# Two attention layers and an MLP on one core: biases as rows, column tiles in one gap, unsummed last weights, another order at the tail

## The chip, the core and the metric

The kernel runs on one core of a Trainium2 chip, in float32. A core has four compute engines that run side by side, each with its own instruction stream in program order: TensorE (PE) multiplies matrices, VectorE (DVE) works elementwise and reduces, ScalarE (ACT) evaluates functions such as exp, GpSimd (POOL) does small elementwise work. SyncE (SP) issues data transfers (DMAs); ACT and POOL issue some too. Data lies in SBUF; TensorE writes to PSUM, which has eight banks of 2 KB per partition, and the other engines read it from there. Engines wait for each other by semaphores.

The metric is the device time of one execution in microseconds; lower is better.

## The reference

Input x is 16 images of 256 channels and 32 x 32 positions, taken as 16 batches of 1024 tokens (S) with 256 channels (C).

```
# layer 0: attention, 4 heads of 64
qkv  = (xs @ w_proj + b_proj).reshape(B, S, 4, 192);  q, k, v = split(qkv, 3)
res  = softmax(q @ k.T * 64**-0.5) @ v
x    = res @ w_out + b_out + xs
# layer 1: attention with 8 heads of 32, then an MLP
qkv  = group_norm(x, 32 groups) @ qkv_w.T
attn = softmax(q @ k.T * 32**-0.5 + phys_bias[head]) @ v
x    = x + attn @ proj_w.T + proj_b
h    = gelu(group_norm(x) -> mlp_w1 (1024 hidden) + mlp_b1) -> mlp_w2 + mlp_b2
out  = x + h
```

## The kernel before

A batch is worked through in stages, and all of TensorE's products are in float32. The tokens are cut into NT = 2 blocks of TB = 512 columns, the channels into CC = 2 halves of 128 rows. In each batch:

- **qk_a, v_a** (L279, the helper `product`, called from qkv): layer 0's projections. ACT evicts them from PSUM with the bias `bqk` added (L715). They are computed during the batch before, except for batch 0, where they are the first thing that TensorE does.
- **Attention of layer 0** (`attention_a`): scores `s_a` (L336) in tiles of 64 x 64, exponentials `e_a` on ACT (L344), products with v `acc_a` (L357), running sums of the exponentials `es_a` on DVE (L369), and the denominators `den_a` (L388), which are products of the sums with ones, in tiles of 128 x 32. The output projection is `o` (`out_proj`, L279), with DVE adding bias and residual (L606) and taking statistics (L609).
- **The gap**: the last acc_a, the o of the first block in two halves with den_a between them, then whatever fills TensorE until the last denominators are through (the next batch's qk_a and v_a in batch 0, the MLP's hidden layer of the batch before in the others).
- **Group norm** g, then **qk_b, v_b**.
- **Attention of layer 1** (`attention_b`): four items (block, channel half), each in four units of two key blocks: scores `s_b` (L468), exponentials `e_b` (L483), products `acc_b` (L519), whose results DVE or ACT adds into `res_b` (L532, L530), sums `es_b` of the exponentials on DVE (L498), at the end of an item the denominators `den_b` (L541) from the sums, and the output projection `j` (L279).
- **Group norm** h, and the **MLP**: hidden `m` (L802) with gelu on ACT (L810), outputs `m` (L279) in eight pieces, of which two make a block of 128 x 512; DVE adds bias and residual (L825) and SP stores (L829).

PSUM is divided by hand: three double banks that rotate (`wide`) and two single banks. Bank 0 takes one head's scores and acc, bank 1 another head's scores and den.

Most stages are generators that yield once per unit. `run(stage, fill)` goes through one and places pieces of other work (`fill`: projections of the next batch, the MLP's output pieces of the one before) after chosen units. `later.after(n, f)` calls f after n more ticks, and there is a tick per unit or piece: this is how the norm's steps (`gm` for the group means, `gv` for the variances) are placed between others. Order on an engine is thus program order, but for DVE and ACT instructions that the scheduler moves unless they are pinned.

`cols[0]` is the width of product()'s column tiles: 128 is one matmul on the whole array, 32 is four matmuls on four column strips of it. It is 32 in both attentions and 128 between them.

At the start ACT's DMA queue issues three loads of `wp` (L92), `pb` (L140) and four of the pieces of `bqk` (L143); SP issues x, two of bqk (L145) and the other weights (L147). The pieces of bqk are columns: every element is 4 bytes of its own. `exp_bias` (L169, L170) turns pb into `ebias` and spreads it to `eones`. At the tail, in batch 15, three of batch 14's eight output pieces stand behind the attention; `keep_warm` (L267) issues idle matmuls while the last norm's small products are waited for. A flag, `in_range`, is taken from the sums of all denominators by a transpose `ok_row` (L967) and two DVE steps; every engine loads it (L188) and branches past `general_pass`, a second version of the kernel that does not run here.

Of the kernel before, what the change touches and what calls it, by code (L numbers as in the profile page):

```python
# [8 lines left out]
F32 = mybir.dt.float32  # L9
# [44 lines left out]
@with_exitstack  # L54
def kernel(
    ctx: ExitStack,
    tc: tile.TileContext,
    x: bass.AP,
    w_proj: bass.AP,
    b_proj: bass.AP,  # L60
    w_out: bass.AP,
    b_out: bass.AP,
    gn1_w: bass.AP,
    gn1_b: bass.AP,
    gn2_w: bass.AP,
    gn2_b: bass.AP,
    qkv_wT: bass.AP,
    proj_wT: bass.AP,
    proj_b: bass.AP,
    phys_bias: bass.AP,  # L70
    mlp_w1T: bass.AP,
    mlp_b1: bass.AP,
    mlp_w2T: bass.AP,
    mlp_b2: bass.AP,
    out: bass.AP,
):
    nc = tc.nc
    B, C, S = x.shape
    HID = mlp_w1T.shape[1]
    CC = C // P  # L80
    SB = S // P
    NT = S // TB
    HC = HID // P
    GSZ = C // GROUPS

    const = ctx.enter_context(tc.tile_pool(name="const", bufs=1))


    wp = const.tile([P, CC, 3, HEADS0, D0], F32, name="wp")
    for t in (1, 0, 2):  # L90
        for cc in range(CC):
            (nc.gpsimd if cc else nc.scalar).dma_start(  # L92
                wp[:, cc, t],
                w_proj[cc * P : (cc + 1) * P, :].rearrange(
                    "p (h t d) -> p t h d", t=3, d=D0
                )[:, t],
            )


    bqk = const.tile([P, 3, HEADS0 // 2], F32, name="bqk")  # L100
    pb = const.tile([P, HEADS1], F32, name="pb")

    ident = const.tile([P, P], F32, name="ident")
    make_identity(nc, ident)
    mhalf = const.tile([P, CC], F32, name="mhalf")
    nc.gpsimd.memset(mhalf, -0.5)
    ones = const.tile([P, D0], F32, name="ones")
    nc.gpsimd.memset(ones, 1.0)

    def load_vec(v, n, name):  # L110
        t = const.tile([P, n], F32, name=name)
        nc.gpsimd.dma_start(t, v.rearrange("(c p) -> p c", p=P))
        return t

    bo = load_vec(b_out, CC, "bo")
    g1w = load_vec(gn1_w, CC, "g1w")
    g1b = load_vec(gn1_b, CC, "g1b")
    g2w = load_vec(gn2_w, CC, "g2w")
    g2b = load_vec(gn2_b, CC, "g2b")
    pjb = load_vec(proj_b, CC, "pjb")  # L120
    m1b = load_vec(mlp_b1, HC, "m1b")
    m2b = load_vec(mlp_b2, CC, "m2b")

    def load_mat(w, name):
        k, n = w.shape
        t = const.tile([P, k // P, n], F32, name=name)
        weights.append((t, w.rearrange("(c p) n -> p c n", p=P)))
        return t

    weights = []  # L130
    wo = load_mat(w_out, "wo")
    wq = load_mat(qkv_wT, "wq")
    wpj = load_mat(proj_wT, "wpj")
    w1 = load_mat(mlp_w1T, "w1")
    w2 = load_mat(mlp_w2T, "w2")


    def load_rest():
        bp = b_proj.rearrange("(g i t d) -> i t d g", i=2, t=3, d=D0)
        nc.scalar.dma_start(pb, phys_bias.partition_broadcast(P))  # L140
        for t in (1, 0):
            for i in range(2):
                nc.scalar.dma_start(bqk[i * D0 : (i + 1) * D0, t, :], bp[i, t])  # L143
        for i in range(2):
            nc.sync.dma_start(bqk[i * D0 : (i + 1) * D0, 2, :], bp[i, 2])  # L145
        for t, w in weights:
            nc.sync.dma_start(t, w)  # L147


    gind = const.tile([P, P // GSZ], F32, name="gind")  # L150
    nc.vector.tensor_reduce(
        gind, ident.rearrange("p (g j) -> p g j", j=GSZ), AX.X, ALU.add
    )
    gavg = const.tile([P, P // GSZ, GSZ], F32, name="gavg")
    nc.vector.tensor_scalar(
        gavg,
        gind.unsqueeze(2).to_broadcast([P, P // GSZ, GSZ]),
        1.0 / GSZ,
        None,
        ALU.mult,  # L160
    )
    gavg = gavg.rearrange("p g j -> p (g j)")


    ebias = const.tile([P, HEADS1], F32, name="ebias")
    eones = const.tile([P, HEADS1, D1], F32, name="eones")

    def exp_bias():
        nc.scalar.activation(ebias, pb, AF.Exp)  # L169
        nc.vector.tensor_copy(eones, ebias.unsqueeze(2).to_broadcast([P, HEADS1, D1]))  # L170

    bvo = const.tile([P, CC], F32, name="bvo")

    in_range = const.tile([P, 1], I32, name="in_range")

    with ExitStack() as first:
        first_pass(
            first, tc, x, out,
            dict(
                wp=wp, bqk=bqk, pb=pb, bo=bo, g1w=g1w, g1b=g1b, g2w=g2w,  # L180
                g2b=g2b, pjb=pjb, m1b=m1b, m2b=m2b, wo=wo, wq=wq, wpj=wpj, w1=w1,
                w2=w2, ident=ident, gavg=gavg, mhalf=mhalf, ones=ones, eones=eones,
                bvo=bvo, load_rest=load_rest, exp_bias=exp_bias,
                in_range=in_range,
            ),
        )

    good = nc.values_load(in_range[0:1, 0:1], min_val=0, max_val=1)  # L188
    with tc.If(good == 0):
        with ExitStack() as again:  # L190
            general_pass(
                again, tc, x, out,
                dict(
                    wp=wp, bqk=bqk, pb=pb, bo=bo, g1w=g1w, g1b=g1b, g2w=g2w,
                    g2b=g2b, pjb=pjb, m1b=m1b, m2b=m2b, wo=wo, wq=wq, wpj=wpj, w1=w1,
                    w2=w2, ident=ident, gavg=gavg, mhalf=mhalf, b_proj=b_proj,
                ),
            )


def first_pass(ctx, tc, x, out, k):
# [62 lines left out]
    def keep_warm(what, n):  # L264
        ps = bank("warm", 1)
        for _ in range(n):
            nc.tensor.matmul(  # L267
                ps[:, : what.shape[1]], what[:, :P], what, start=True, stop=True
            )
# [52 lines left out]
    def attention_a(b, qT, kT, v, project):  # L322
# [102 lines left out]
        while pending:  # L425
            weigh(*pending.pop(0))
            if not pending:


                cols[0] = P  # L430
                first_half = project(0, res)
                first_half((0,))
                yield
                first_half((1,))
                break
            yield

# [6 lines left out]
    def attention_b(b, qT, kT, v, project):  # L444
# [41 lines left out]

        def add(i, kb, es, block):
            if kb == 0 and block == 0:  # L490
                sums[i] = [
                    work.tile([P, 2, TB], F32, tag="es", name=f"es_{key}_{i}_{n}", bufs=4)
                    for n in range(G // 2)
                ]
                return
            for n in range(G // 2):
                d = sums[i][n]
                ins = nc.vector.tensor_add(d, es[n] if kb == 0 else d, es[2 * block + n])  # L498
                if block:
                    tc.keep_in_program_order(ins)  # L500
# [35 lines left out]
        def normalise(i, r, last):  # L536
            t, c = items[i]
            at_end = last and b == B - 1
            den = bank(f"den_{key}_{i}", 1)
            for g in range(G):  # L540
                nc.tensor.matmul(  # L541
                    den[g * D : (g + 1) * D, :],
                    k["eones"][:, c * G + g],
                    sums[i][g // 2][:, g % 2, :],
                    start=True,
                    stop=True,
                )
            if at_end:

                full = work.tile([P, CC * TB], F32, tag="full", name="rd_end", bufs=1)  # L550
# [44 lines left out]
    def out_proj(key, w, src, bias, xs, t, stats, then):  # L595
        todo = list(range(CC))

        def issue(cos=range(CC)):
            apart = cols[0] == P
            if not apart:  # L600
                both = wide(f"{key}_{t}")
            ps = {}
# [27 lines left out]
        return issue  # L630


    def group_norm(key, src, stats, gw, gb, tag, out_tile, wait, at_end=False):
        st = {}


# [22 lines left out]
        def variances():  # L659
# [1 line left out]
            for sl, ps in averages(f"gm_{key}", st["mean_c"]):  # L661
                nc.vector.tensor_copy(mean[sl], ps)

            if at_end:
                keep_warm(k["ident"], 4)
            dv = small.tile([P, CC], F32, tag="dv", name=f"dv_{key}")
            nc.vector.tensor_sub(dv, st["mean_c"], mean)
            nc.vector.tensor_mul(dv, dv, dv)
# [5 lines left out]
        def apply():  # L674
            rstd = small.tile([P, CC], F32, tag="rstd", name=f"rstd_{key}")
            for sl, ps in averages(f"gv_{key}", st["tv"]):
                nc.vector.tensor_scalar(rstd[sl], ps, EPS, None, ALU.add)
            if at_end:
                keep_warm(k["ident"], 10)
            nc.gpsimd.tensor_tensor(rstd, rstd, k["mhalf"], ALU.pow)  # L680
            a = small.tile([P, CC], F32, tag="ga", name=f"ga_{key}")
            nc.vector.tensor_mul(a, rstd, gw)
# [113 lines left out]
    def mlp(b, xb, hn):  # L796
# [16 lines left out]
        def reduce(t, co, half):  # L813
# [11 lines left out]
            nc.vector.scalar_tensor_tensor(  # L825
                y, ps, k["m2b"][:, co : co + 1], y, ALU.add, ALU.add
            )
            if half:
                nc.sync.dma_start(  # L829
                    out[b, co * P : (co + 1) * P, t * TB : (t + 1) * TB],  # L830
                    xb[:, co, t * TB : (t + 1) * TB],
                )

        return (
            [lambda t=t, hc=hc: hidden(t, hc) for t in range(NT) for hc in range(HC)],
# [29 lines left out]
    keep_warm(nothing, 3)  # L865
    xs = {0: load_x(0)}
    k["load_rest"]()
    tiles0, (first_qk, first_v) = qkv_0(0, xs[0])

    run_pieces(first_qk[::2] + first_qk[1::2] + first_v)  # L870
    k["exp_bias"]()


# [16 lines left out]
    for b in range(B):  # L890
# [31 lines left out]
            first = []  # L922
        if b == B - 1:

            now, end = outputs[:5], outputs[5:]
        if not first:

            fill = {m: [piece] for m, piece in enumerate(own[:5:2] + own[1::2] + own[6:])}
# [11 lines left out]
        for m, pieces in enumerate(rest):  # L940
# [4 lines left out]
                b, tiles1, xs[b],  # L945
                lambda st, b=b, hn=hn: group_norm(
                    f"h{b}", xs[b], st, k["g2w"], k["g2b"], "q1", hn,
                    3 if b + 1 < B else 2, b == B - 1,
                ),
            ),  # L950
            fill,
# [305 lines left out]
```

## Time and profile before

| what | us |
|---|---|
| median of 4 runs | 3775.19 |
| lowest, highest | 3773.49, 3776.57 |
| profiled execution, its own time | 3774.78 |
| its span in the profile | 3772.9 |
| TensorE busy | 3757.0 |
| DVE busy | 2231.4 |
| ACT busy | 2034.2 |
| POOL busy | 78.0 |

The profiled execution is one of the kind that the four runs are; its time is its span and 1.9 us around it. Times within it count from the span's start. In lines of groups or of the timeline, `x16` is a number of instructions, "128\*32" the shape of the part of the array that a matmul uses, "out<-in" the tiles by name, and a bracket the idle time of the engine before the line and what ended it. In the list of waits the three numbers are the time in total, how often, and the longest. In the timeline, matmuls of one kind are merged, and the first number is the start, the second the time from the first start to the last end; a next line can start before that end, since matmuls overlap. In the chain, "ACTq" is a DMA that ACT issues.

### The profile page before, as it was taken

Reading aid. Unit: us, or ns where it says so; the run is one execution under the profiler, and the core shown is the slowest. Engines: PE = TensorE matmul, PEld = TensorE weight load, DVE = VectorE, ACT = ScalarE, POOL = GpSimd, SP = SyncE. Lnnn points to the kernel's source line nnn. Section 1 sums busy time; section 2 is a strip of 40 time slices with the busy share of each in tenths; the row PEclk is TensorE's granted clock in tenths of the full one; section 3 lists DMA queues with packets and bytes.
Section 4 is the critical chain, followed back from the end, with each engine's and each line's share of the span. In section 5 each row is a group of like instructions: output and inputs, shape, how many; then the busy total and the mean of one; then the engine's idle time right before and its main releaser. Section 6 shows DMA issues by size and latency. Waiting matters only on the chain.

```text
span 3772.9 us, 86793 instructions
## 1 busy us (share of the span) xinstructions
PE 3757.0 (100%) x38335; PEld 1491.4 (40%) x38335; DVE 2231.4 (59%) x2764; ACT 2034.2 (54%) x2624; POOL 78.0 (2%) x245
## 2 busy tenths in 40 slices
PE   9999999999999999999999999999999999999999
PEld 3334343343433434334343333433334333343335
DVE  4684656746566565665656656565565655646573
ACT  4655546555465554555546455554655556555461
POOL 1000000000000000000000000000000000000000
PEclk9999999999999999999999999999999999999999
DMA  2000000000001000000000001010000100100000
GB/s 85 12 14 13 30 13 16 27 13 30 12 16 32 7 30 13 19 29 8 30 13 23 26 10 31 8 33 15 13 30 7 33 15 13 30 7 22 15 12 22
DMA packets 63052, 78.27 MB, mean 21 GB/s; under 512 B 35820, under 2 KB 37356, under 8 KB 62668
## 3 DMA queue, kind: packets, MB, share of 16 engines
q1 hardware_dynamic: 59964, 71.85, 6.2%
q8 instruction: 302, 4.95, 0.5%
q14 instruction: 82, 0.67, 0.1%
q10 hardware_dynamic: 2304, 0.40, 0.1%
q0 software_dynamic: 400, 0.41, 0.1%
HBM read 54.28 MB, written 17.56 MB: 19 GB/s over the span
## 4 chain that ended last, share of the span: by engine, by line
PE 97%; DVE 1%; issue 1%; ACT 1%; DMA 0%; ACTq 0%; POOLq 0%; POOL 0%; DVEq 0%
PE s_b L468 13%; PE acc_b L519 12%; PE m L802 12%; PE m L279 12%; PE s_a L336 12%; PE acc_a L357 11%; PE qk_b L279 6%; PE qk_a L279 6%; PE o L279 3%; PE v_b L279 3%; PE v_a L279 3%; PE j L279 3%; PE den_b L541 1%; PE den_a L388 1%; DVE es_a L369 0%
## 5 line engine op out<-in xcount | busy, mean ns | idle before, releaser
L483 ACT ACTIVATE e_b<-s_b 128x1024 f32<-128x1024 f32 (+1 forms) x1280 | 982.6, 865 | 471.2 <-PE s_b L468 471.2
L498 DVE TENSOR_TENSOR es_b<-es_b,e_b 128x1024 f32<-128x1024 f32 x768 | 900.1, 1221 | 337.5 <-ACT e_b L483 337.4
L344 ACT ACTIVATE e_a<-s_a 128x1024 f32<-128x1024 f32 x512 | 521.2, 1025 | 359.8 <-PE s_a L336 349.4
L468 PE MATMUL s_b<-q,k 32*64 32x512 f32 x8192 | 535.8, 601 | 4.0 <-DVE res_b L532 3.3
L336 PE MATMUL s_a<-q,k 64*64 64x512 f32 x4096 | 532.6, 593 | 1.1
L357 PE MATMUL acc_a<-e_a,v 64*64 64x512 f32 x4096 | 528.5, 589 | 0.0
L369 DVE TENSOR_TENSOR es_a<-es_a,e_a 128x1024 f32<-128x1024 f32 x384 | 469.3, 1222 | 85.4 <-ACT e_a L344 73.4
L519 PE MATMUL acc_b<-e_b,v 128*32 128x512 f32 x4096 | 492.1, 598 | 0.0
L279 PE MATMUL m<-g,w 128*32 128x256 f32 (+1 forms) x7664 | 464.1, 379 | 0.0
L802 PE MATMUL m<-gn_h,w 128*128 128x512 f32 x1024 | 451.3, 595 | 0.3 <-DVE gn_h L692 0.3
L810 ACT ACTIVATE g<-m,m1b 128x512 f32<-128x512 f32 x256 | 175.9, 687 | 358.3 <-PE m L802 358.3
L279 PEld LDWEIGHTS m<-g,w 128*32 128x32 f32 (+1 forms) x7664 | 276.7, 112 | 216.8 <-issue 41.9
L468 PEld LDWEIGHTS s_b<-q,k 32*64 32x64 f32 x8192 | 174.2, 130 | 288.7 <-issue 147.1
L802 PEld LDWEIGHTS m<-gn_h,w 128*128 128x128 f32 x1024 | 192.2, 190 | 230.6 <-issue 229.8
L357 PEld LDWEIGHTS acc_a<-e_a,v 64*64 64x64 f32 x4096 | 161.9, 133 | 277.5 <-issue 236.2
L336 PEld LDWEIGHTS s_a<-q,k 64*64 64x64 f32 x4096 | 152.6, 133 | 278.1 <-issue 211.8
L519 PEld LDWEIGHTS acc_b<-e_b,v 128*32 128x32 f32 x4096 | 108.5, 109 | 351.1 <-ACT e_b L483 194.7
L532 DVE TENSOR_TENSOR res_b<-res_b,acc_b 128x512 f32<-128x512 f32 x192 | 131.2, 683 | 196.2 <-PE acc_b L519 196.2
L279 PE MATMUL qk_a<-x,wp 128*32 128x512 f32 (+1 forms) x1856 | 231.6, 592 | 3.7 <-ACT q L715 1.8
L279 PE MATMUL qk_b<-gn_g,wq 128*32 128x512 f32 (+1 forms) x1280 | 234.0, 592 | 0.0
L736 DVE TENSOR_TENSOR v<-v_b,eones 128x512 f32<-128x512 f32 x64 | 44.0, 688 | 291.2 <-PE v_b L279 291.2
L498 DVE TENSOR_TENSOR es_b<-e_b,e_b 128x1024 f32<-128x1024 f32 x128 | 150.6, 1218 | 0.0
(121 smaller groups left out, 2094.7 us busy)
## 6 DMA issues: line engine op xcount, KB each, us to landing
rd_a<-row_a SPq DMA_DIRECT2D x64, 256.0 KB
out_dram<-x SPq DMA_DIRECT2D x64, 256.0 KB
rd_b<-row_b SPq DMA_DIRECT2D x252, 64.0 KB
x<-in_x_dram SPq DMA_DIRECT2D x30, 512.0 KB
w<-in_L_conv_mlp_w_dram SPq DMA_DIRECT2D x2, 1024.0 KB
x<-in_x_dram SPq DMA_DIRECT2D x4, 256.0 KB
sp_b<-d_b SPq DMA_DIRECT2D x63, 8.0 KB
row_b<-inv_b SPq DMA_DIRECT2D x63, 8.0 KB
```

What stands on the lines that cost most here:

```text
L279: nc.tensor.matmul(o[sl], w[:, sl], r, **flags)
L336: nc.tensor.matmul(s[h : h + HALF, g, :], kT[g * D : (g + 1) * D, c, kb * P + h : kb * P + h + HALF], qT[g * D : (g + 1) * D, c, t * TB : ...
L344: nc.scalar.activation(e, s, AF.Exp, scale=float(D) ** -0.5)
L357: nc.tensor.matmul(accs[i][h][g * D : (g + 1) * D, :], v[h * HALF : (h + 1) * HALF, kb, c * 2 + g], e[h * HALF : (h + 1) * HALF, g, :], st ...
L369: nc.vector.tensor_add(sums[i], held[i] if kb == 1 else sums[i], e)
L468: nc.tensor.matmul(outs[g][h : h + HALF, :], kT[g * D : (g + 1) * D, c, k0 : k0 + HALF], qT[g * D : (g + 1) * D, c, t * TB : (t + 1) * TB] ...
L483: nc.scalar.activation(to, s, AF.Exp, scale=float(D) ** -0.5)
L498: ins = nc.vector.tensor_add(d, es[n] if kb == 0 else d, es[2 * block + n])
L519: nc.tensor.matmul(acc[g * D : (g + 1) * D, :], v[:, kb + m, c * G + g], es[2 * m + g // 2][:, g % 2, :], start=(m == 0), stop=(m == 1),)
L532: nc.vector.tensor_add(r, r, acc)
L802: nc.tensor.matmul(ps, k["w1"][:, cc, hc * P : (hc + 1) * P], hn[0][:, cc, t * TB : (t + 1) * TB], start=(cc == 0), stop=(cc == CC - 1),)
L810: nc.scalar.activation(g, ps, AF.Gelu, bias=k["m1b"][:, hc : hc + 1])
```

## The change

Four parts:

1. **Biases as rows.** The six loads of bqk columns go. Three loads bring b_proj as rows, `brow` (6 x 128), on ACT's queue between wp's second third (t = 1) and the others. TensorE turns it (a transpose to 128 x 6 in bank 0, placed behind the first two k tiles) and DVE copies it to bqk. The order of the first four tiles on TensorE becomes k, k, transpose, q, q, where it was k, q, k, q.
2. **Column tiles in the gap.** o's two halves in the gap use 128 x 32 tiles, each in a bank of its own as before; the width changes to 128 only after them.
3. **Last weights unsummed.** For items 2 and 3 of batch 0 and item 3 of batch 15 (`spared`), the last unit's exponentials are not added to the sums; den_b takes their four tiles as further rounds of its accumulation.
4. **Tail.** In batch 15 four of the output pieces stand in the attention and four behind it, where it was five and three; the last norm waits one tick less, so that its gm and gv stand between those pieces; the idle matmuls go. The last block of the output is stored in two halves. On all engines the flag's steps (ok_row and what follows from it) stand behind the last output piece, where they stood in front of the last MLP.

```diff
     wp = const.tile([P, CC, 3, HEADS0, D0], F32, name="wp")
+    brow = const.tile([3 * HEADS0 // 2, P], F32, name="brow")
     for t in (1, 0, 2):
+        if t == 0:
+            bp = b_proj.rearrange("(g i t d) -> t g i d", i=2, t=3, d=D0)
+            for u in range(3):
+                nc.scalar.dma_start(
+                    brow[u * 2 : (u + 1) * 2].rearrange("g (i d) -> g i d", d=D0), bp[u]
+                )
...
     def load_rest():
-        bp = b_proj.rearrange("(g i t d) -> i t d g", i=2, t=3, d=D0)
         nc.scalar.dma_start(pb, phys_bias.partition_broadcast(P))
-        for t in (1, 0):
-            for i in range(2):
-                nc.scalar.dma_start(bqk[i * D0 : (i + 1) * D0, t, :], bp[i, t])
-        for i in range(2):
-            nc.sync.dma_start(bqk[i * D0 : (i + 1) * D0, 2, :], bp[i, 2])
...
+                first_half = project(0, res)
+                first_half((0,), True)
+                yield
+                first_half((1,), True)
                 cols[0] = P
-                first_half = project(0, res)
-                first_half((0,))
-                yield
-                first_half((1,))
                 break
...
+        spared, apart = {0: (2, 3), B - 1: (3,)}.get(b, ()), {}
         def add(i, kb, es, block):
...
+            if i in spared and kb == SB - 2:
+                apart[i] = es
+                return
...
             den = bank(f"den_{key}_{i}", 1)
-            for g in range(G):
-                nc.tensor.matmul(
-                    den[g * D : (g + 1) * D, :],
-                    k["eones"][:, c * G + g],
-                    sums[i][g // 2][:, g % 2, :],
-                    start=True,
-                    stop=True,
-                )
+            parts = sums[i] + apart.get(i, [])
+            for m in range(0, len(parts), G // 2):
+                for g in range(G):
+                    nc.tensor.matmul(
+                        den[g * D : (g + 1) * D, :],
+                        k["eones"][:, c * G + g],
+                        parts[m + g // 2][:, g % 2, :],
+                        start=(m == 0),
+                        stop=(m + G // 2 == len(parts)),
+                    )
...
-        def issue(cos=range(CC)):
-            apart = cols[0] == P
+        def issue(cos=range(CC), apart=False):
+            apart = apart or cols[0] == P
...
-            if at_end:
-                keep_warm(k["ident"], 4)
...
-            if at_end:
-                keep_warm(k["ident"], 10)
...
-            if half:
-                nc.sync.dma_start(
-                    out[b, co * P : (co + 1) * P, t * TB : (t + 1) * TB],
-                    xb[:, co, t * TB : (t + 1) * TB],
-                )
+            each = b == B - 1 and (t, co) == (NT - 1, CC - 1)
+            if half or each:
+                sl = slice(t * TB + (half * n if each else 0), t * TB + (half + 1) * n)
+                nc.sync.dma_start(out[b, co * P : (co + 1) * P, sl], xb[:, co, sl])
...
     k["load_rest"]()
+    ps, n = bank("bqk", 0), k["brow"].shape[0]
+    turn = nc.tensor.transpose(ps[:, :n], k["brow"], k["ident"][:n, :n])
+    nc.vector.tensor_copy(k["bqk"].rearrange("p t g -> p (t g)"), ps[:, :n])
     tiles0, (first_qk, first_v) = qkv_0(0, xs[0])
-    run_pieces(first_qk[::2] + first_qk[1::2] + first_v)
+    start = first_qk[::2] + first_qk[1::2] + first_v
+    start[0]()
+    with tc.issue_after(turn.ins):
+        start[1]()
+    run_pieces(start[2:])
...
-            now, end = outputs[:5], outputs[5:]
+            now, end = outputs[:4], outputs[4:]
...
-                    3 if b + 1 < B else 2, b == B - 1,
+                    3 if b + 1 < B else 1,
```

More of the change, by code (lines that the diff above doesn't have):

```diff
@@ L182 @@
                 w2=w2, ident=ident, gavg=gavg, mhalf=mhalf, ones=ones, eones=eones,
-                bvo=bvo, load_rest=load_rest, exp_bias=exp_bias,
+                bvo=bvo, brow=brow, load_rest=load_rest, exp_bias=exp_bias,
                 in_range=in_range,
@@ L630, in out_proj, with group_norm @@
         return issue
-    def group_norm(key, src, stats, gw, gb, tag, out_tile, wait, at_end=False):
+    def group_norm(key, src, stats, gw, gb, tag, out_tile, wait):
         st = {}
```

## The prediction

> **What bounds the kernel now.** I read the page first: engine table, then the chain that ended last.
>
> ```profile
> PE 3757.0 (100%) x38335; PEld 1491.4 (40%) x38335; DVE 2231.4 (59%) x2764; ACT 2034.2 (54%) x2624; POOL 78.0 (2%) x245
> ...
> PE 97%; DVE 1%; issue 1%; ACT 1%; DMA 0%; ACTq 0%; POOLq 0%; POOL 0%; DVEq 0%
> ```
>
> TensorE is busy for 3757.0 of 3772.9 us, so 15.9 us of the span is not matmul. An edit pays if it takes passes from TensorE (one 512-column pass takes 0.43 us start to start), bubbles between passes, or part of those 15.9 us; relief on DVE or ACT is worth nothing where TensorE runs through. The waits of TensorE say where it doesn't:
>
> ```profile
> PE s_b L468 <- DVE res_b L532: 3.3, 6, 0.9
> PE qk_a L279 <- ACT q L715: 1.8, 1, 1.8
> PE qk_a L279 <- ACT k L715: 1.6, 1, 1.6
> ```
>
> The two of qk_a are the start. The chain of the first 26 us:
>
> ```profile
> 2.12 7.84 DMA wp<-in_L_conv_w_proj_dram
> 9.96 0.02 issue
> 9.98 0.60 ACTq L143
> ...
> 10.62 5.88 DMA bqk<-in_L_conv_b_proj_dram
> ...
> 16.61 0.70 ACT q L715
> ...
> 17.35 7.13 PE qk_a L279 x16
> ```
>
> ACT's third bqk load waits on a completion semaphore that the wp load shares (9.96), the last lands at 16.50, and TensorE stands: by the timeline 2.26 us (11.27 to 13.53), then 2.10 us (15.25 to 17.35). qk_a ends at 24.48.
>
> **Part 1, biases as rows.** Six loads of 4-byte pieces become three of four 256-byte pieces, ahead of two wp loads on ACT's queue; SP loses two, so wo, wq and the later loads go about 2 us sooner. An issue on that queue takes 0.60 to 0.67 us. Three put wp t=0 from 1.42 to about 3.4 and pb from 2.81 to about 4.9, where it also waits for the x block that lands at 4.89. Queue data is served in order and wp t=1 before it only lands at 4.72, so I leave wp t=0 at its landing of 7.8 and pb at its 10.2 (both read from the completion records); brow, with so few pieces and between the two, before 7 by estimate.
>
> The new order on TensorE: k, k from 5.66 to about 9.2, the transpose (which waits for brow and the identity, nothing later), q to about 11.1, then the fourth tile. It needs the first k eviction on ACT, which now waits for the bqk copy. On DVE that copy stands behind eones (waits ebias on ACT, which waits pb) and gind: pb 10.2, ebias 0.21, eones 0.29, gind 0.28, copy about 0.2: 11.4. The ACT_TABLE_LOAD (1.28) fits before pb lands. Eviction 0.69: the fourth tile starts at 12.3. No second stall follows, and the remaining five tiles take 5 x 1.72 = 8.6: end 20.9. To that I add 0.7 for hand-overs between engines and for wo and wq, which now share the DMA engines with pb: 21.6. Gain **2.9 us**. Bounds: pb landing 3 us later gives nothing (the copy would be at 14.4); pb early gives at most the 4.4 us of stalls.
>
> **Part 2, column tiles in the gap.** Once per batch, in time order:
>
> ```profile
> 88.72 1.98 PE L279 MATMUL o<-res_a,wo 128*128 128x512 f32 x4
> 90.63 1.07 PE L388 MATMUL den_a<-es_a,ones 128*32 128x256 f32 x16
> 91.63 1.98 PE L279 MATMUL o<-res_a,wo 128*128 128x512 f32 x4
> 93.45 2.74 PE L279 MATMUL qk_a<-x,wp 128*128 128x512 f32 x6
> ```
>
> Four passes are 1.72 us, yet o to den_a takes 1.91, den_a's 0.86 take 1.00 and the second o 1.82: each change of tile shape costs 0.09 to 0.11, and the first 128x128 pass after one takes 0.105 more (o: 592 median, 697 longest, ns). With 128x32 tiles o, den_a, o have one shape: 1.72 + 0.86 + 1.72 and one change plus slow pass at the end, 0.21: 4.52 against 93.45 - 88.72 = 4.73. Saved 0.21 x 16 = **3.3 us**.
>
> Against it stands a rule of the Trainium skill (TensorEngine Tiling (Array Packing), Instruction Overhead): each matmul carries about 60 cycles. The halves go from 8 records to 32 per batch; at the clock of 2.4 GHz that the skill gives (TensorE: Matmul & The Clock Gate) 24 x 25 ns x 16 = 9.6 us lost by estimate, net 6.3 lost. The row: the same product j, in both forms.
>
> ```profile
> 213.71 3.62 PE L279 MATMUL j<-res_b,wpj 128*32 128x512 f32 x32
> ...
> 3697.58 3.60 PE L279 MATMUL j<-res_b,wpj 128*128 128x512 f32 x8
> ```
>
> 24 more instructions cost 0.02 us, since four column tiles run side by side (starts 7 ns apart). I take the row: 0.3 us over 16 batches, within rounding. Range 2.3 to 3.6.
>
> **Part 3, the last weights unsummed.** Per item it drops four DVE adds (two rows of 2.35) and adds four rounds of den_b: 4 x 0.43 = 1.72 us on TensorE. Batch 0, item 2:
>
> ```profile
> 191.33 2.35 DVE L498 TENSOR_TENSOR es_b<-es_b,e_b 128x1024 f32<-128x1024 f32 x2
> ...
> 193.60 0.68 DVE L532 TENSOR_TENSOR res_b<-res_b,acc_b 128x512 f32<-128x512 f32 x1
> ...
> 194.34 1.97 PE L468 MATMUL s_b<-q,k 32*64 32x512 f32 x30 [0.92 <-DVE res_b L532]
> ...
> 197.98 1.04 PE L541 MATMUL den_b<-es_b,eones 128*32 128x512 f32 x8
> ```
>
> Without the adds res_b runs at 192.5 and the 0.92 stall goes; then den_b takes 1.72 more and everything behind it (s_b, d_b's copy, e_b) moves: +0.8. Item 3 has no stall after its spared adds (TensorE runs without a gap from 210.07 to 219.83 and on): +1.72. Its earlier 0.43 stall at 210.07 follows exponentials that come later by the same 0.8; it stays. Sum **2.4 us lost**. Bounds: if the freed DVE also removed the 0.43 and more of the stalls it would be 1.5 lost; if the chain of DVE steps (186 to 210, on the chain of this stretch) shortens by all 4.7 us of item 2's adds, 1.3 gained. e_b tiles are held until den_b, but the exponentials that reuse them come after it. Batch 15's item is in part 4.
>
> **Part 4, the tail.** Before, acc_b of 3682.71 to the first hidden matmul of the last MLP:
>
> ```profile
> 3709.95 2.03 PE L267 MATMUL warm<-ident 128*128 128x128 f32 x16
> ...
> 3712.29 1.99 PE L802 MATMUL m<-gn_h,w 128*128 128x512 f32 x4 [0.31 <-DVE gn_h L692]
> ```
>
> That is 29.6 us. After, TensorE has in this order: acc 1.72, j 3.43, acc 1.72, den 0.97 + 1.72, m 3.45, j 3.43, m 3.43, gm, m 3.43, gv, m 3.43, small products and switches 0.6: 27.4. Each step's cover: the 3.36 RECIPROCAL and the scaling of the last result lie under the first m and half of j (a stall of 0.2 at most); bn_stats to mean_c (2.65 after j) under the second m; gm to tv_h (0.9) under the third; rstd to gn_h (2.2) under the last. With that cover gone the 2.2 would be bare. Gain 29.6 - 27.4 = **2.1 us** (0.5 to 3), the 1.72 of den included. Removing the warm matmuls has a rule against it (clock-gate page, Part 1: an idle window of about 3.4 us halves the clock; worth about 3.4 us once). The granted clock is 1.00 there, and the new order leaves no such gap, so I add nothing.
>
> The very end:
>
> ```profile
> 3767.68 0.48 DVE L825 SCALAR_TENSOR_TENSOR x<-m,m2b,x 128x256 f32<-128x256 f32 x1 [2.97 <-PE m L279]
> 3768.20 0.33 SPq L829 DMA_DIRECT2D out_dram<-x  x1
> ```
>
> The store lands at 3771.02, but by the raw records DVE ends the span: it loads the flag by 3768.24, branches, and its next instruction comes 3.5 us later (3771.83). Now ok_row's transpose, least (0.28), cast (0.14) and the flag's load (0.5) follow the last x on all engines: the branch goes about **1.0 us later** (0 to 2). Halving the last store can't help: the landing is not last.
>
> **Sum.** -2.9 - 3.3 + 2.4 - 2.1 + 1.0 = -4.9. The profiled execution (3774.78, span 3772.9) becomes 3769.9; it stood 0.4 under the median of 3775.19, so the median becomes **3770.3**.
>
> **Rivals.** (a) *Larger gain*, 0.22: batch 0 is paced by DVE, whose relief gains 1.3 instead of 2.4 lost (the DVE steps on the chain speak for it, the unbroken TensorE after 210 against), and the start gets all 4.4: -4.9 - 3.7 - 1.5 = -10.1: 3765.1. (b) *Start and tail don't pay*, 0.14: pb lands 3 us late and the norm's chain stays bare: -4.9 + 2.9 + 2.1: 3775.3. pb's wait for an earlier load speaks for it, its small share of the queue against. (c) *Slower*, 0.02: the instruction overhead of 60 cycles holds in the gap: 9.6 us there, 3780 in all; it outweighs all gains from 13 ns per extra matmul and passes +0.2% from 32 ns. The j rows (0.8 ns) speak against.
>
> **How the numbers follow.** 0.2% is 7.55 us, about what a measurement of this kernel can tell from no change (the four runs spread over 3.1). The forecast has 0.62, at 3768 to 3773. (a) lies mostly beyond 3767.6, (b) within. Faster 0.23, within 0.75, slower 0.02. The range takes in (b)'s middle part and most of (a): 3765.5 to 3774.5.
>
> **What would show it.** qk_a ends near 21.6 with one stall, its releaser ACT k (pb late: after 24). o x16 at 1.72 with den_a next at 0.86. den_b at 2.6 in batch 0, with the 0.92 wait gone. Hidden's start in the last MLP 27.4 after acc, no warm. DVE's in_range after the last x. The forecast falls if den_b's rounds cost less than 0.43 each or if batch 0's attention as a whole gets shorter.

## The result and the profile after

The changed kernel takes 3770.27 us (median of 40 runs, 3768.8 to 3774.06) against 3774.4 us of the kernel before in the same sessions (60 runs): ratio 0.9988, 95% interval 0.9983 to 0.9992, about 4 us. The profiled execution took 3770.62 us, its span is 3768.8 us, 4.1 us under that of before.

The engine table of the page and the waits of TensorE (engine and line, released by; total, times, longest):

```profile
PE 3755.8 (100%) x38692; PEld 1485.3 (39%) x38692; DVE 2218.2 (59%) x2753; ACT 2034.3 (54%) x2624; POOL 77.9 (2%) x245
```

```profile
PE s_b L470 <- DVE res_b L541: 2.4, 5, 0.7
PE warm L269 <- DVE nothing L871: 1.5, 1, 1.5
PE qk_a L281 <- ACT k L722: 0.6, 1, 0.6
```

TensorE is as full as before. Of the two waits of qk_a one is left, the stall of 0.9 us in batch 0 is gone from s_b's list, and so is a wait of 0.3 us for gn_h in the tail. Where the 4.1 us come from is read by laying both timelines side by side at fixed points of TensorE's order:

| stretch | before | after | difference | forecast |
|---|---|---|---|---|
| span's start to first v_a | 24.32 | 21.88 | -2.44 | -2.9 |
| to the first s_a of batch 1 (one gap, batch 0's unsummed items) | 195.51 | 197.54 | +2.03 | -0.2 + 2.4 |
| to the first o of batch 15 (14 gaps) | 3325.01 | 3322.23 | -2.78 | -2.9 |
| to the first hidden matmul of the last MLP (one gap, the tail) | 167.44 | 165.10 | -2.34 | -0.2 - 2.1 |
| that MLP on TensorE | 55.36 | 55.26 | -0.10 | 0 |
| from its last matmul to the end | 5.27 | 6.76 | +1.49 | +1.0 |
| sum | 3772.9 | 3768.8 | -4.1 | -4.9 |

The start, by the chain of the changed kernel's first 26 us:

```profile
5.41 6.19 DMA pb<-in_L_conv_phys_bias_dram
...
11.62 0.22 ACT ebias L171
11.84 0.02 issue
11.86 0.29 DVE eones L172
12.16 0.19 DVE gind L153
12.35 0.08 DVE bqk L877
...
12.46 0.70 ACT k L722
...
13.20 8.85 PE qk_a L281 x20
22.05 4.10 PE v_a L281 x19
```

The order is the predicted one, pb, ebias, eones, gind, bqk, eviction, fourth tile; pb comes later than assumed.

The gap, in time order:

```profile
86.28 1.92 PE L281 MATMUL o<-res_a,wo 128*32 128x512 f32 x16
88.02 1.05 PE L390 MATMUL den_a<-es_a,ones 128*32 128x256 f32 x16
88.89 1.90 PE L281 MATMUL o<-res_a,wo 128*32 128x512 f32 x16
90.72 9.71 PE L281 MATMUL qk_a<-x,wp 128*128 128x512 f32 x22
```

o to den_a takes 1.74, den_a 0.86, the second o 1.83 with the one change of shape that is left: 4.43 (4.74 before), in every one of the 16 batches. Of these 0.30 us, 0.10 comes back in the first 128x128 pass, so 0.20 per batch stay (2.78 over 14 gaps).

Batch 0's second attention:

```profile
194.24 1.04 PE L552 MATMUL den_b<-es_b,eones 128*32 128x512 f32 x8
195.10 1.90 PE L552 MATMUL den_b<-e_b,eones 128*32 128x512 f32 x16
196.93 2.74 PE L470 MATMUL s_b<-q,k 32*64 32x512 f32 x32
...
217.60 1.90 PE L552 MATMUL den_b<-e_b,eones 128*32 128x512 f32 x16
219.43 2.81 PE L338 MATMUL s_a<-q,k 64*64 64x512 f32 x24
```

The rounds from e_b are the 1.72 us per item (16 records, 1.90 to the end of the last, overlapped by the next). The tail, with gv_h between two pieces of m and no warm:

```profile
3703.09 0.28 PE L281 MATMUL gv_h<-tv_h,gavg 128*128 128x2 f32 x2
3703.22 3.70 PE L281 MATMUL m<-g,w 128*128 128x256 f32 x16
3706.76 9.60 PE L809 MATMUL m<-gn_h,w 128*128 128x512 f32 x22
```

acc_b of 3679.39 to 3706.76 is 27.37 us, where 27.4 was forecast. The very end:

```profile
3761.86 0.27 PE L981 MATMUL ok_row<-ident,both 128*1 128x128 f32 x1
3762.06 0.48 DVE L832 SCALAR_TENSOR_TENSOR x<-m,m2b,x 128x256 f32<-128x256 f32 x1 [2.97 <-PE m L281]
3762.46 0.27 DVE L983 TENSOR_REDUCE least<-ok_row 1x1 f32<-1x128 f32 x1
3762.76 0.14 DVE L984 CAST in_range<-least 1x1 int32<-1x1 f32 x1
```

By the raw records every engine loads the flag at 3762.9 and branches from 3763.5 on.

No line of the diff moves the flag: in both sources its block stands behind `run_pieces(hidden + outputs)`. In the trace of before, `ok_row` runs ahead of the last MLP all the same, between two idle matmuls:

```profile
3709.04 0.27 PE L967 MATMUL ok_row<-ident,both 128*1 128x128 f32 x1
```

So the scheduler moves this product of TensorE too. The kernel with part 4 alone, whose edit does not touch the block either, has it at 3765.81, behind the last piece. It is thus an edit of part 4 that turned the order; which one was not tested.

### The profile page after: what moved, and what is told of

It is laid out like the page before. It is cut to its first block, busy times and chain, and to the rows that moved or that the text cites. A ratio compares the mean times of both kernels' runs of the same rounds, so it can differ in the third digit from the quotient of the medians.

```text
span 3768.8 us, 87484 instructions
## 1 busy us (share of the span) xinstructions
PE 3755.8 (100%) x38692; PEld 1485.3 (39%) x38692; DVE 2218.2 (59%) x2753; ACT 2034.3 (54%) x2624; POOL 77.9 (2%) x245
## 4 chain that ended last, share of the span: by engine, by line
PE 97%; DVE 1%; issue 1%; ACT 1%; DMA 0%; SPq 0%; DVEq 0%
PE s_b L470 13%; PE acc_b L528 12%; PE m L809 12%; PE m L281 12%; PE s_a L338 12%; PE acc_a L359 11%; PE qk_b L281 6%; PE qk_a L281 6%; PE v_b L281 3%; PE o L281 3%; PE v_a L281 3%; PE j L281 3%; PE den_b L552 2%; PE den_a L390 1%; DVE es_a L371 0%
## 5 line engine op out<-in xcount | busy, mean ns | idle before, releaser
L507 DVE TENSOR_TENSOR es_b<-es_b,e_b 128x1024 f32<-128x1024 f32 x756 | 885.9, 1221 | 339.1 <-ACT e_b L485 339.0
```

## The experiments

Below, "in its trace" means between the same fixed points as above, so a difference in the start does not enter another stretch. Kernels that are alike in a stretch agree in it within 0.3 us from trace to trace. Medians are of 6 to 21 runs each, and all kernels with the start of before spread over two groups of times some 2.5 us apart (a likely reason stands under part 1). The intervals of the four parts alone and of the kernel without the adds reach a ratio of 1, no change, so the verdicts on these rest on the stretches of their traces more than on the medians. Theories: **mine**, TensorE's passes and bubbles decide, part by part, and the parts add; **rival A**, DVE's relief in batch 0 is worth more than the passes it costs; **rival B**, an overhead per matmul spoils the gap; **rival C**, start or tail don't reach the end.

**Part 2 alone.** The kernel before with

```diff
+                first_half = project(0, res)
+                first_half((0,), True)
+                yield
+                first_half((1,), True)
                 cols[0] = P
...
```

> The kernel before with part 2 alone (the gap's o in 128x32 tiles, every batch). My account: 0.20 us less per batch, 3.2 us less than before in all; o to the work behind den_a and o takes 4.43 instead of 4.74 us to its first matmul, of which 0.1 comes back in that first matmul. Rival (a fixed cost per matmul of 60 cycles, 384 more matmuls): 6 us more than before.

3770.82 us against 3774.12 (ratio 0.9992, 0.9984 to 1.0000). In its trace, from the first v_a to the last matmul, 3.1 us less than before; the gap 4.43. Mine holds; 384 more matmuls cost nothing that can be seen, so rival B falls: it wanted 6 us more.

**Part 1 alone** (three row loads, the transpose and the copy; the six column loads out).

> The kernel before with part 1 alone (biases as rows). My account: the first qk_a ends 2.4 us earlier and nothing behind it takes that back, since TensorE runs through: 2.4 us less than before. Rival (the start is hidden behind something later): the difference is lost by the first gap, no change in the time.

3772.19 us against 3774.12 (0.9993, 0.9985 to 1.0001). In its trace the first v_a stands at 21.25 instead of 24.32, and the last matmul is 3.0 earlier: nothing is taken back. Rival C falls for the start. The medians differ by 1.9 us only; the trace of before is one execution of a start that varies (see below). The chain of its first 26 us shows that TensorE then has no stall at all in qk_a:

```profile
1.47 5.49 PE warm L268 x6
6.95 3.81 PE qk_a L280 x8
10.76 0.15 PE bqk L870
10.91 10.50 PE qk_a L280 x24
21.41 4.75 PE v_a L280 x22
```

The traces with the start of before do not agree among themselves: the first v_a stands at 24.32, 25.68 (part 2 alone), 23.13 (part 3), 26.22 (part 4) and 23.32 (the last one below). With the new start of part 1 it stands between 20.62 and 21.88 in seven traces. The two latest have the bqk loads late for both evictions, and TensorE idle for 2.74 and 2.65 us at once. Part 2 alone, the stall and then stretches of 2 us (the last three numbers are the granted TensorE clock, the DMA share and GB/s):

```profile
15.30 10.55 PE L279 MATMUL qk_a<-x,wp 128*128 128x512 f32 x20 [2.74 <-ACT k L715]
...
14.00:16.00 2.00, 0.70 (x2) 0.46 (x3) 0.00 (x0) 1.44 (x3) 0.00 (x0) 1.00 1.01 357
16.00:18.00 2.00, 2.00 (x4) 0.88 (x4) 0.00 (x0) 0.62 (x2) 0.00 (x0) 0.67 1.02 398
18.00:20.00 2.00, 2.00 (x3) 0.68 (x2) 0.00 (x0) 0.47 (x1) 0.00 (x0) 0.50 1.10 358
20.00:22.00 2.00, 2.00 (x6) 0.94 (x5) 0.00 (x0) 0.69 (x1) 0.00 (x0) 0.98 1.06 409
```

From 1.4 us after the stall's end the clock is half for 3.4 us, and four passes start 0.85 us apart instead of 0.43: 1.7 us more. In part 4 alone the same 3.4 us begin 0.35 us after a stall of 2.65 us. The longest stall of the other twelve traces here is 1.84 us (before), and none of them has the half clock. The Trainium skill (TensorE: Matmul & The Clock Gate, Part 1) has this rule, half rate after an idle window of about 3.4 us that runs free of the kernel; here stalls of 2.74 and 2.65 us went before it, shorter than that window, after 0.38 and 1.25 us of idle a little earlier. No run varies the stall alone, so the cause is argued from these fourteen traces. Both profiled executions with it lie in the upper group of their kernel's times (part 4 alone: seven runs at 3770.8 to 3771.6, six at 3773.6 to 3775.4, the profiled one 3774.31), the others in the lower. With part 1, 12 of 13 runs lie within 1.2 us. That each run of the upper group has the half clock was not shown run by run, and the new start does not end every spread: the 21 runs of the changed kernel with batch 0 summed again lie over 4.8 us.

**Part 3 alone, in batch 0.**

```diff
+        spared, apart = {0: (2, 3)}.get(b, ()), {}
...
+            if i in spared and kb == SB - 2:
+                apart[i] = es
+                return
...
```

> The kernel before with part 3 alone, for items 2 and 3 of batch 0. My account: 2.3 us more than before: 3.4 us of den_b passes against one stall of 0.9 us that goes. Rival (DVE paces batch 0's second attention and its relief counts): 1 us less than before or better.

3777.08 us against 3774.12 (1.0006, 0.9998 to 1.0014). In its trace the stretch from the first v_a to batch 1 grows by 2.23 us. Rival A falls. To see both halves of the bill apart, the same without den_b's further rounds (its denominators lack the last unit, so it serves for its time only):

> The kernel before without the last unit's four DVE adds in items 2 and 3 of batch 0 and without any further rounds of den_b: the last unit is left out of those denominators. What DVE's relief alone is worth. My account: only the 0.9 us stall in item 2 goes, 0.9 us less than before. Rival (DVE sets the pace from 186 to 210 us): 2.4 to 4.7 us less than before.

3772.92 us against 3774.12 (0.9996, 0.9988 to 1.0005); in its trace that stretch is 1.11 us shorter, where the rival wanted 2.4 or more. Its den_b in item 2 and what follows:

```profile
195.87 1.04 PE L546 MATMUL den_b<-es_b,eones 128*32 128x512 f32 x8
196.86 2.82 PE L468 MATMUL s_b<-q,k 32*64 32x512 f32 x32
...
207.97 1.97 PE L468 MATMUL s_b<-q,k 32*64 32x512 f32 x30 [0.43 <-DVE res_b L537]
```

So eight DVE adds (9.4 us of DVE) are worth 1.1 us, the rounds cost 1.11 + 2.23 = 3.3 us (3.44 forecast), and the 0.43 stall of item 3 stays, as the prediction had it. And undone in the changed kernel:

> The changed kernel with batch 0's last weights summed again (batch 15's still unsummed). My account: 2.3 us less than the changed kernel, 6.4 less than before. Rival (DVE's relief counts): 1 us more than the changed kernel or worse.

3768.48 us against 3774.12 (0.9983, 0.9977 to 0.9990): 5.6 us less than before (6.4 expected), where the changed kernel has 4.1. In its trace the stretch has only the gap's gain, 0.2.

**Part 4 alone, nothing unsummed.**

```diff
-            now, end = outputs[:5], outputs[5:]
+            now, end = outputs[:4], outputs[4:]
...
-                    3 if b + 1 < B else 2, b == B - 1,
+                    3 if b + 1 < B else 1,
...
```

> The kernel before with part 4 alone (four and four pieces, one tick less, no idle matmuls, halved last store), the last weights summed in batch 15 too. My account: the last MLP starts 2.8 us earlier (29.6 less the 27.4 of the changed kernel, less 1.7 for den_b's rounds, plus about 1.1 for a wait of j for the scaled result); the end after the last matmul grows by 1.5 us, since the flag is now read behind it: 1.2 us less than before. Rival (the tail pays as a whole, the end is free): 2.8 us less.

3771.61 us against 3774.12 (0.9994, 0.9985 to 1.0002). In its trace the last MLP starts 3.4 us earlier after the first o of batch 15 than before (2.8 expected) and the end grows by 1.3. By the medians this is 2.5 us less than before, twice what was expected and near the rival's 2.8, but not for the rival's reason: the end is not free. Of the expected wait of j for the scaled result, 1.1 us, only 0.24 is there: the scheduler puts the first passes of the next m into it.

```profile
3696.00 1.02 PE L279 MATMUL j<-res_b,wpj 128*128 128x512 f32 x2
3696.86 0.59 PE L279 MATMUL m<-g,w 128*128 128x256 f32 x2
3697.69 2.81 PE L279 MATMUL j<-res_b,wpj 128*128 128x512 f32 x6 [0.24 <-DVE part L555]
```

Batch 15's unsummed weights so have next to no stall to pay for them. All weights summed in the changed kernel:

> The changed kernel with all last weights summed. My account: batch 15's rounds cost 1.7 us of TensorE and save about 1.1 us of a wait of j for the scaled result, so this is 0.6 us faster than the one with batch 0 alone undone. Rival (the sparing is worth it where the reciprocal is waited for): it is 0.5 us or more slower than that one.

3767.29 us against 3774.12 (0.9981, 0.9973 to 0.9988), 1.2 under the one before; in its trace the tail, without its gap's 0.2, is 3.4 us shorter than before, with batch 15's rounds 2.2. Unsumming costs 1.2 us there, and 2.2 in batch 0.

**The flag ahead of the last MLP**, in the changed kernel (the block of `ok`, `ok_row`, `least` moved above this line):

```diff
     later.flush()
+    ...
     run_pieces(hidden + outputs)
```

> The changed kernel with the flag's steps (ok_row, least, in_range) written ahead of the last MLP. My account: the end after the last matmul returns to that of the kernel before, 5.2 us instead of 6.7, at 0.2 us for the transpose: 1.3 us less than the changed kernel. Rival (the last store's landing sets the end): at most 0.5 us less.

3769.26 us against 3774.12 (0.9987, 0.9980 to 0.9994), 1.0 under the changed kernel's median of other sessions. In its trace the end after the last matmul is 4.72 us instead of 6.76, 2.0 less. The medians show less of it: the profiled execution, 3767.24, is the fastest of its 20. With all weights summed the same move is worth 2.2 us by the medians (6.8 us under before without it, 9.0 with it, below). When TensorE loads the flag, in the changed kernel and in this one (the numbers before the ";" are the first and last start):

```profile
L190 PEldq TENSOR_LOAD <-in_range x1: 495/495/495, 3762.9 to 3762.9; - x1
...
L190 PEldq TENSOR_LOAD <-in_range x1: 490/490/490, 3756.7 to 3756.7; - x1
```

The raw records say why it is more than the 1.05 us by which DVE's branch moved: with the flag known early, TensorE branches while its last matmuls are still running (at 3757.32; they end at 3760.75) and its 3.70 us until the next instruction are hidden; in the changed kernel it branches at 3763.54 and needs 4.12 us, more than DVE's 3.1, and ends the span. The rival (the last store's landing) falls: it allowed 0.5 us.

**Together.**

> The changed kernel once more, beside the next two. My account: 4 us less than before; the first v_a starts between 20.6 and 21.9 us, as in the runs that share this start.

> The changed kernel with all last weights summed and the flag's steps ahead of the last MLP. If the parts add: 2.2 + 1.2 + 1.9 = 5.3 us less than the changed kernel, 9 less than before. Rival (the parts overlap): 3.5 us less than the changed kernel or not as much.

The changed kernel again: 3770.36 us against 3773.95 (0.9990, 0.9983 to 0.9996), first v_a at 21.01. With all weights summed and the flag early: 3764.93 us (0.9977, 0.9967 to 0.9986), 5.4 under it (5.3 expected): these two add. The four parts alone (-1.9, -3.3, +3.0, -2.5 by the medians) and batch 15's rounds (+1.2) come to -3.5 us, where the changed kernel has -4.1.

> The same, with pb loaded on POOL's queue right behind its first third of wp instead of on ACT's behind all of wp. My account: the bqk copy then waits for the transpose and no longer for pb; the wait of TensorE for the first k eviction (0.2 to 0.6 us) goes, 0.4 us less than the kernel without this. Rival (POOL's later wp loads come late for q): 0.5 us more.

3763.83 us (0.9973, 0.9962 to 0.9983). pb is there at 6.6 and the bqk copy follows the transpose at once, yet the first v_a stands at 20.97 (21.12 with pb on ACT's queue): TensorE already ran through qk_a in that trace, as it did with part 1 alone. The 1.1 us of the medians are not explained by these two traces; with pb's landing no longer in the chain its lateness in other executions would be taken out, but that was not shown. What stands ahead of the first k tile then are the idle matmuls, which start 0.85 us apart, at half rate. One of the three less:

```diff
-    keep_warm(nothing, 3)
+    keep_warm(nothing, 2)
```

> The kernel with pb on POOL's queue, with two instead of three idle matmuls at the very start. With pb gone from the chain the first k tile starts when those idle matmuls end (6.75 us), which run at half rate. My account: the first k tile starts at about 5.2, waits once for POOL's first wp load (6.5), and the first v_a starts 0.5 to 1 us earlier than with three: 20.2 instead of 21.0. Rival (the clock's rise comes as much later): no change or 1 us more.

3763.36 us against 3773.87 (0.9970, 0.9958 to 0.9982). The first v_a moves to 20.25, 0.7 earlier; the clock rises at 6.96 us, where it rose at 7.02, so it does not come later in this trace. The expected wait for POOL's load of wp does not show.

```profile
1.47 3.78 PE L269 MATMUL warm<-nothing 128*128 128x512 f32 x4 [1.47 <-DVE nothing L871]
5.21 4.55 PE L281 MATMUL qk_a<-x,wp 128*128 128x512 f32 x8
9.70 0.22 PE L876 MATMUL bqk<-ident,brow 6*128 6x6 f32 x1
9.85 10.57 PE L281 MATMUL qk_a<-x,wp 128*128 128x512 f32 x24
```

This is the fastest of all: 10.5 us under before of its own session, where the changed kernel is 4.1 under.

## Why the prediction was right, point by point

The median came out at 3770.27 where 3770.3 was forecast. That is closer than the sum deserves: the kernel before read 3774.4 over more runs, not 3775.19, and the gain is 4.1 us, not 4.9. By its steps:

- **Gap, -3.3.** Right: 0.20 per batch, 3.1 in all. Weighing the rule of 60 cycles per matmul against the row of j decided this, and the row was right. One of its terms was small: den_a took 0.14 us more than its 0.86, where 0.09 to 0.11 stood for a change of shape.
- **Batch 0, +2.4.** Right in size (2.2) and in both halves: 3.3 for the rounds, 1.1 for the adds. Its own terms, 0.8 and 1.72, add up to 2.5, not 2.4. The rival that DVE paces this stretch rested on DVE steps in the chain; a chain names what came last at each wait, not how far behind it the next one was. Here taking 9.4 us of adds from DVE brought TensorE forward by 1.1 us only.
- **Tail, -2.1.** Right: 2.15, with each cover as named. Of the 3.4 us that the order brings without batch 15's rounds, these took 1.2; the prediction had them in its sum (at 1.72), but not as something to leave out. It put the half clock that the idle matmuls guard against at 3.4 us once; where it came, in the start of part 2 alone, it cost 1.7. Here the clock stayed at 1.00 without them.
- **Start, -2.9.** The chain was right, two of its terms were not. pb landed at 11.6, not 10.2 (in the other traces of this start ebias ran at 10.4 to 10.8, so the assumed landing was nearly right for those). And the k tiles did not start at 5.66 but at 6.75: the idle matmuls before them run at half rate and ended later than in the trace of before. The prediction took that time from one execution; in others of the same start it is 5.5 to 6.8. Without pb's lateness the fourth tile could not have begun before 12.4 in this trace either. Its reading of the old start was off as well: the brackets of the timeline give TensorE's two stalls as 1.58 and 1.84 us, not 2.26 and 2.10, so an early pb could bring 3.4 us at most, not 4.4.

```profile
13.53 1.99 PE L279 MATMUL qk_a<-x,wp 128*128 128x512 f32 x4 [1.58 <-ACT k L715]
...
17.35 7.13 PE L279 MATMUL qk_a<-x,wp 128*128 128x512 f32 x16 [1.84 <-ACT q L715]
```

  This did not enter the sum, which counts from the end of qk_a. The fourth tile began at 13.20, 0.9 us later than forecast, and the 0.7 us set aside for hand-overs, which did not come (8.68 us for the rest, 8.6 forecast), made up for most of it: that is luck. What the prediction did not see is that the old start sometimes also loses 1.7 us to the clock.
- **End, +1.0.** Right for DVE's branch (1.72 us after the last matmul, 0.67 before: +1.05), too small in all (+1.5), since only DVE was followed. DVE's next instruction comes only 0.64 later, as its branch took 3.10 us instead of 3.51. TensorE's branch had begun at 3764.22, under the last matmuls (they end at 3767.65); moved behind them it needs 4.12 us and becomes the last. In the two kernels with weights summed again the two engines come within 0.2 us of each other.

Rival (a)'s larger gain is there, but not where it was sought: not in DVE's relief, but in leaving the unsummed weights out and in an early flag.

## What to carry to other kernels

Where TensorE is full, price every edit in its passes and in the bubbles between tile shapes first; an engine that is relieved only gives back the stall in which TensorE waited for it, here 1.1 us for 9.4 us of VectorE's adds. Keep products of one tile shape together, and read a cost per instruction from a row of the same product in both forms. Work that decides a branch belongs ahead of the last long stretch, so that all engines can jump while it runs; follow each engine to its own end, not only the one that was last before.

## What the runs showed of the hardware

- Stalls of TensorE of 2.74 and 2.65 us near 13 to 16 us were followed, 1.4 and 0.35 us after their end, by 3.4 us at a granted clock of 0.50 (four passes at 0.85 us instead of 0.43); in the twelve traces whose stalls are 1.84 us or less the clock stayed at 1.00 once it had risen.
- From the branch at the kernel's end to the next instruction of its own queue TensorE took 3.5 to 4.2 us and DVE 3.0 to 3.7 over the fourteen traces; for TensorE this is hidden where it branches while its earlier matmuls still run (3757.32, last matmul to 3760.75).
- The three idle matmuls at the start took 4.23 to 5.49 us from execution to execution, as the clock rose at 4.3 us in one and at 7.6 in another; what stands behind them in order moves with that.
- With o on 128x32 tiles, the shape of den_a between its halves, and four matmuls in place of one, the gap took 4.43 instead of 4.74 us in each of 16 batches; the first 128x128 pass after a change of shape took 0.10 us more than the next.
